# Mask operations pinned in program order, half of the early masks moved beside h, and separate buffers for u

**Chip, cores, metric.** One core of one Trainium2 chip. The metric is the device time in microseconds (us) of that core. The kernel before takes 2171.65 us, the median of its four runs beside the changed kernel (2167.68 to 2175.49). Every run that this document compares is of the fast state, except one single look whose state is unknown, which is marked. A ratio is the mean time of one kernel's fast runs over the mean time of the other's fast runs of the same rounds, so it is not quite the ratio of the medians that are quoted.

## The reference

Two layers of a graph network on 4096 nodes with 512 features, adjacency `adj` 4096 x 4096 in float32:

```python
xw  = max(sign(x), 0) @ sign(W0).T                 # binary weights
x   = layernorm(x + relu(adj @ xw))                # "aggregation"
node_att = softmax(x @ node_w, axis=0)
h   = x @ edge_w                                   # "h"
e   = where(adj > 0, h @ h.T, -9e15)               # "scores e"
att = node_att * softmax(e, axis=1)
x   = layernorm(x + adj * att @ (x @ weight) + bias)   # "final product"
```

The places where `adj` is not positive have to be known when the scores are made. Part of these masks is made early: a piece of `adj` (128 rows x 1024 columns, 512 KB) is loaded, turned into bf16 zeros and large negative numbers (256 KB), and stored in a DRAM tensor `mask_d`, from which the stage of e reads it later. There are 80 such early pieces. The rest of `adj` is loaded and masked during e.

## The kernel before

A compiler with a scheduler orders the instructions of each engine. It may move an operation ahead of others that stand before it in the program, unless that operation is pinned with `keep_in_program_order`. Names: PE is TensorE, DVE is VectorE, ACT is ScalarE, POOL is GpSimd, SP is SyncE. "The wire" is what the DMA engines can carry together; the DMA share is the mean share of time in which they were busy, and the clock is the granted clock of PE as a share of full speed.

The aggregation takes blocks of 128 rows of `adj_t`. Each block has two halves of two quarters. ACT makes a high part `hi` of a quarter, DVE the remainder `lo`, and PE multiplies both:

```python
pieces = deque((r, j, c) for r in range(NG) for j in range(BG) for c in range(0, r + 1, 2))   # 80
bufs = deque([pair[:, 0, :], pair[:, 1, :], single])       # three buffers of 512 KB
def premask():
    if loaded and (len(loaded) == 2 or not pieces):
        (r, j, c), a = loaded.popleft()
        m = a.bitcast(BF16)...[:, :, :W]                   # the mask lies in the piece's own buffer
        nc.vector.tensor_scalar(m, a..., 0.0, NEG_BIG, ALU.is_le, ALU.mult)
        nc.gpsimd.dma_start(mask_d[r][:, c : c + 2, j, :], m)
        bufs.append(a)
    if pieces:
        r, j, c = pieces.popleft()
        a = bufs.popleft()
        nc.gpsimd.dma_start(a, adj[ts(r * BG + j, P), c * W : (c + 2) * W])
        loaded.append(((r, j, c), a))

def aggregate(b):
    ...
    for half in range(2):
        nc.sync.dma_start(at, adj_t[b, :, ts(half, HB), :])       # 1 MB
        for q in range(2):
            nc.scalar.copy(hi, aq)
            nc.vector.tensor_sub(lo, aq, hi.bitcast(F32))
            if (half, q) != (0, 0):
                premask()
            ... 16 matmuls of hi and lo against xw, into acc
    nc.vector.scalar_tensor_tensor(xb, acc, 0.0, xb, ALU.max, ALU.add)
    layernorm([xb]); ... sums and stores on GpSimd ...
```

Before it stands the head: the product `xw`, with the first two blocks beside it, whose loads `a` shared four buffers (`rows`) with `u`, an intermediate result of the binary product. After it stands h, a dense run of 56 groups of matmuls in which the DMA engines had next to nothing to do (11 GB/s at a share of 0.03).

Of the kernel before, what the change touches and what calls it, by code (L numbers as in the profile page):

```python
# [11 lines left out]
F32 = mybir.dt.float32  # L12
# [3 lines left out]
ALU = mybir.AluOpType  # L16
AX = mybir.AxisListType

P = 128
EPS = 1e-5  # L20
NEG_BIG = -(2.0**53)
# [7 lines left out]
def kernel(  # L29
# [13 lines left out]
    nc = tc.nc  # L43
    N, D = x.shape
    NB = N // P
    KD = D // P
    W = 512
    NG = N // W
    BG = W // P
# [7 lines left out]
    rows = ctx.enter_context(tc.tile_pool(name="rows", bufs=4))  # L57
# [98 lines left out]
    with (  # L156
# [15 lines left out]
        def whole(g):  # L172

            xt = stream.tile([P, KD, W], F32, name="xt", tag="stream")
            ba = wp.tile([P, KD, W // 2], F32R, name="ba", tag="quarter", bufs=2)
            pws = [ps_mm.tile([P, D], F32, name="pw", tag="mm") for j in range(BG // 2)]
            order = [(k, j) for j in range(BG // 2) for k in range(KD)]

            def signs(k, over):
                a, b = xt[:, k, : W // 2], xt[:, k, W // 2 :]  # L180
                nc.vector.tensor_scalar(over, b, 0.0, TWO, ALU.is_gt, ALU.mult)
                nc.vector.scalar_tensor_tensor(ba[:, k, :], a, 0.0, over, ALU.is_gt, ALU.add)

            if g == 0:

                pos = sp.tile([P, KD, D], BF16, name="pos", tag="lo")
                over = sp.tile([P, KD, W // 2], F32, name="over0", tag="hi")
                for k in range(KD):
                    nc.sync.dma_start(w0[:, k, :], w0_t[ts(k, P), :])
                    nc.scalar.dma_start(xt[:, k, :], x_t[ts(k, P), ts(g, W)])  # L190
                for _ in range(WARM):
                    nc.tensor.matmul(pws[0], warm[:, :P], warm, start=True, stop=True)
                for k in range(KD):
                    nc.vector.tensor_scalar(pos[:, k, :], w0[:, k, :], 0.0, None, ALU.is_gt)
                    signs(k, over[:, k, :])
                    nc.vector.scalar_tensor_tensor(bw[:, k, :], w0[:, k, :], 0.0, pos[:, k, :], ALU.is_lt, ALU.subtract)
                order = [(k, j) for k in range(KD) for j in range(BG // 2)]
            else:
                nc.sync.dma_start(xt, x_t[:, ts(g, W)].rearrange("(k p) n -> p k n", p=P))
                over = sp.tile([P, KD, W // 2], F32, name="over0", tag="hi")  # L200
                nc.vector.tensor_scalar(over, xt[:, :, W // 2 :], 0.0, TWO, ALU.is_gt, ALU.mult)
                nc.vector.scalar_tensor_tensor(ba, xt[:, :, : W // 2], 0.0, over, ALU.is_gt, ALU.add)
            for k, j in order:
                nc.tensor.matmul(pws[j], ba[:, k, ts(j, P)], bw[:, k, :], start=(k == 0), stop=(k == KD - 1))
                if k == KD - 1:

                    u = rows.tile([P, D], F32, name="u", tag="rows")
                    nc.scalar.activation(u, pws[j], AF.Identity, bias=shift[:, 0:1])
                    b = g * BG + j
                    nc.vector.scalar_tensor_tensor(xw[:, b, :], u, SHIFT, pws[j], ALU.subtract, ALU.subtract)  # L210
                    nc.scalar.activation(xw[:, b + BG // 2, :], u, AF.Identity, bias=shift[:, 1:2], scale=-1.0 / TWO)
# [38 lines left out]



        pieces = deque((r, j, c) for r in range(NG) for j in range(BG) for c in range(0, r + 1, 2))
        pair = wp.tile([P, 2, 2 * W], F32, name="pair", tag="we_s")
        single = wp.tile([P, 2 * W], F32, name="single", tag="quarter", bufs=2)
        sums_l = wp.tile([P, 4, HD], F32, name="sums_l", tag="quarter", bufs=2)
        bufs = deque([pair[:, 0, :], pair[:, 1, :], single])
        loaded = deque()

        def premask():  # L260

            if loaded and (len(loaded) == 2 or not pieces):
                (r, j, c), a = loaded.popleft()

                m = a.bitcast(BF16).rearrange("p (c w) -> p c w", c=2)[:, :, :W]
                nc.vector.tensor_scalar(m, a.rearrange("p (c w) -> p c w", c=2), 0.0, NEG_BIG, ALU.is_le, ALU.mult)  # L266
                nc.gpsimd.dma_start(mask_d[r][:, c : c + 2, j, :], m)
                bufs.append(a)
            if pieces:
                r, j, c = pieces.popleft()  # L270
                a = bufs.popleft()
                nc.gpsimd.dma_start(a, adj[ts(r * BG + j, P), c * W : (c + 2) * W])
                loaded.append(((r, j, c), a))


        def aggregate(b):
            xb = rows.tile([P, D], F32, name="xb", tag="rows")
            nc.sync.dma_start(xb, x[ts(b, P), :])
            acc = accs[early.index(b)] if b in early else ps_mm.tile([P, D], F32, name="acc", tag="mm")
            for half in range(0 if b in early else 2):  # L280
                at = stream.tile([P, HB, P], F32, name="at", tag="stream")
                nc.sync.dma_start(at, adj_t[b, :, ts(half, HB), :])

                for q in range(2):
                    aq = at[:, ts(q, QC), :]
                    hi = sp.tile([P, QC, P], F32R, name="hi", tag="hi")
                    nc.scalar.copy(hi, aq)  # L287
                    lo = sp.tile([P, QC, P], F32R, name="lo", tag="lo")
                    nc.vector.tensor_sub(lo, aq, hi.bitcast(F32))  # L289
                    if (half, q) != (0, 0):  # L290
                        premask()
                    for c in range(QC):
                        kb = half * HB + q * QC + c
                        nc.tensor.matmul(acc, hi[:, c, :], xw[:, kb, :], start=(kb == 0), stop=False)  # L294
                        nc.tensor.matmul(acc, lo[:, c, :], xw[:, kb, :], start=False, stop=(kb == NB - 1))  # L295
            nc.vector.scalar_tensor_tensor(xb, acc, 0.0, xb, ALU.max, ALU.add)
            layernorm([xb])
            scr = wp.tile([P, D], F32, name="scr")
            nc.vector.tensor_tensor_reduce(
                scr, xb, nw_b, 1.0, 0.0, ALU.mult, ALU.add, accum_out=node_s[:, b : b + 1]  # L300
            )
            nc.gpsimd.tensor_add(scr, xb, bias_b)
            nc.gpsimd.dma_start(x1_d[ts(b, P), :], scr)
            return xb
# [22 lines left out]
        for n in range(NB):  # L327
            b = n // 2 + n % 2 * HB
            xb = aggregate(b)
            if n == NB - 3:  # L330
                assert not loaded
                we_s = wp.tile([P, KD, D], F32, name="we_s")
                nc.sync.dma_start(we_s, edge_w.rearrange("(k p) o -> p k o", p=P))
            if n % 2:
                left(n // 2, before[1], xb)
            if before is not None:
                transpose_rows(*before)
            before = (b, xb)
# [12 lines left out]
        nc.gpsimd.tensor_sub(s3, l11, l21)  # L351
        nc.gpsimd.tensor_sub(s4, l12, s2)
        left_h = l11, l12, s4, l22, s1, s2, s3
        for g in range(HG):
            r11, r12 = (x1T[:, :HK, ts(c, W)] for c in (g, g + HG))
            r21, r22 = (x1T[:, HK:, ts(c, W)] for c in (g, g + HG))
            t1, t2 = (sp.tile([P, HK, W], F32, name="t12", tag="hi") for _ in range(2))
            t3, t4 = (sp.tile([P, HK, W], F32, name="t34", tag="lo") for _ in range(2))
            nc.vector.tensor_sub(t1, r12, r11)
            nc.gpsimd.tensor_sub(t3, r22, r12)  # L360
            nc.vector.tensor_sub(t2, r22, t1)
            nc.vector.tensor_sub(t4, r21, t2)
            right_h = r11, r21, r22, t4, t1, t2, t3
            seven(
                lambda m, q: [left_h[m][:, k, ts(q, P)] for k in range(HK)],
                lambda m: [right_h[m][:, k, :] for k in range(HK)],
                [[hT[:, q + f, ts(c, W)] for f in (0, HK) for c in (g, g + HG)] for q in range(2)],
                lambda *_: None,
            )


    nmax = const.tile([P, 1], F32, name="nmax")
# [98 lines left out]
    class Rows:  # L471
# [24 lines left out]
        def row(self, i, s, src):  # L496
            b, c = self.r * BG + i, self.c
            if self.i is None:
                e = Uses(1, free_e)
                line, mask = e.buf, self.mask[:, i, :]  # L500
            else:
                e = self.a
                line = mask = e.buf.rearrange("p c w -> p (c w)")
                nc.vector.tensor_scalar(mask, mask, 0.0, NEG_BIG, ALU.is_le, ALU.mult)  # L504
            nc.vector.tensor_tensor_reduce(  # L505
                line, mask, src, -1.0, HUGE, ALU.add, ALU.min, accum_out=nmax_c[:, b, c : c + 1]
            )
# [534 lines left out]
```

## Time and profile before

The stages are cut at the first or last matmul of each; the head ends where DVE takes over the first accumulator after the two early blocks.

| stage | us | what limits it |
|---|---|---|
| head | 103.2 | PE 77 us busy, waits for `hi` |
| aggregation | 583.2 | 16 blocks of 24.1 us with four or five masks each (72 in all), then 15.0 us per block |
| h | 96.4 | PE |
| e | 495.6 | PE, idle 20 us |
| final product | 894.6 | PE |
| span of the profiled execution | 2173.0 | |

The prediction below shows the windows, the waits of PE and DVE in the aggregation, and one stall. Three more answers matter. The last two I used in the prediction; the first I had not weighed. It is what GpSimd waited for between 103.2 and 489.5 us (total us, times, longest):

```profile
POOL pair L272 <- DMA mask_d<-pair: 80.1, 24, 8.9
POOL single L272 <- DMA mask_d<-single: 36.1, 8, 7.7
```

Both lines say that GpSimd, about to issue the load of a piece, stood until the store of the mask out of the same buffer had landed: 116 us of 386. In the longest of these waits, the 8.87 us before 114.56 us, the trace shows no instruction of GpSimd start: what stands behind such a load waits too. Then the head (PE, 0 to 103 us) and the stage of e (DVE, 783 to 1278 us):

```profile
PE acc L234 <- ACT hi L224: 17.0, 8, 7.5
```
```profile
DVE lent L504 <- DMA lent<-in_adj_dram: 91.6, 36, 5.8
```

### The profile page before, as it was taken

What the parts mean: (1) busy time and instruction counts of PE and PEld (TensorE: products, weight loads), DVE (VectorE), ACT (ScalarE), POOL (GpSimd) and SP (SyncE); (2) the same over time, 40 slices, a digit from 0 to 9 for tenths busy, and PEclk for the clock granted to TensorE, in tenths of its full rate; (3) what the DMA queues carried; (4) which work ended last, traced back from release to release, by engine and by line L of the source; (5) the groups of instructions that cost most, each with busy time, mean ns of one, the idle gap of its engine ahead of it and who ended that gap; (6) DMA issues with size and microseconds to landing.
All of it is one profiled execution on the core that took longest, in us unless ns stands there. A gap on an engine that the chain in (4) does not pass through costs nothing.

```text
span 2173.0 us, 18035 instructions
## 1 busy us (share of the span) xinstructions
PE 2015.5 (93%) x6108; PEld 1119.2 (52%) x6108; DVE 1340.4 (62%) x1896; ACT 672.3 (31%) x1107; POOL 555.7 (26%) x683
## 2 busy tenths in 40 slices
PE   6867767779999999989999989999999999999997
PEld 4646656657886444544454544444444444444443
DVE  5544444535556545746674668778777867686734
ACT  3411212222332035756665752112111211121100
POOL 0345444543334100111111221124022411241101
PEclk8988988889999999999999999999999999999999
DMA  6778888787662045856784987776667665766531
GB/s 232 252 273 283 282 276 289 272 277 249 205 210 84 0 160 189 287 207 240 267 296 159 363 313 283 247 259 227 238 208 278 229 230 208 274 245 232 174 106 58
DMA packets 133644, 497.70 MB, mean 229 GB/s; under 512 B 14000, under 2 KB 14000, under 8 KB 125872
## 3 DMA queue, kind: packets, MB, share of 16 engines
q0 software_dynamic: 83008, 304.12, 38.9%
q1 hardware_dynamic: 49968, 191.39, 26.7%
q8 instruction: 48, 0.79, 0.1%
q10 hardware_dynamic: 576, 1.05, 0.1%
q14 instruction: 44, 0.36, 0.0%
HBM read 376.96 MB, written 119.54 MB: 228 GB/s over the span
## 4 chain that ended last, share of the span: by engine, by line
PE 46%; DMA 4%; issue 3%; DVE 2%; POOL 0%; ACT 0%; POOLq 0%; DVEq 0%
PE ps L828 35%; PE seven L642 5%; PE po L881 4%; DMA s_d<-slot 1%; DMA lent<-in_adj_dram 1%; DVE line L505 1%; DMA s_d<-lent 1%; PE pt L543 1%; DMA lent<-in_adj_t_dram 0%; DMA slot<-in_adj_t_dram 0%; DVE lent L505 0%; DMA xb<-x_d 0%; ACT line L514 0%; DVE lent L504 0%; POOL s_d L659 0%
## 5 line engine op out<-in xcount | busy, mean ns | idle before, releaser
L295 PE MATMUL acc<-xw,lo 128*128 128x512 f32 x960 | 402.3, 419 | 101.2 <-DVE lo L289 101.1
L828 PE MATMUL ps<-lent,lop 128*128 128x512 f32 x992 | 432.6, 592 | 0.0
L294 PE MATMUL acc<-xw,hi 128*128 128x512 f32 x960 | 397.4, 414 | 0.0
L828 PE MATMUL ps<-slot,lop 128*128 128x512 f32 x800 | 351.9, 594 | 0.0
L828 PEld LDWEIGHTS ps<-lent,lop 128*128 128x128 f32 x992 | 188.3, 190 | 236.3 <-issue 231.3
L295 PEld LDWEIGHTS acc<-xw,lo 128*128 128x128 f32 x960 | 194.1, 202 | 158.1 <-DVE lo L289 116.4
L828 PEld LDWEIGHTS ps<-slot,lop 128*128 128x128 f32 x800 | 152.2, 191 | 190.1 <-issue 185.4
L287 ACT CAST hi<-at 128x1024 fp32r<-128x1024 f32 x120 | 125.8, 1048 | 304.0 <-PE acc L294 296.3
L294 PEld LDWEIGHTS acc<-xw,hi 128*128 128x128 f32 x960 | 194.1, 202 | 40.7
L289 DVE TENSOR_TENSOR lo<-at,hi 128x1024 fp32r<-128x1024 f32 x120 | 153.8, 1284 | 57.4 <-ACT hi L287 57.3
L832 DVE TENSOR_TENSOR over<-over,ps 128x512 f32<-128x512 f32 x168 | 113.3, 680 | 92.4 <-PE ps L828 92.4
L266 DVE TENSOR_SCALAR pair<-pair 128x1024 bf16<-128x1024 f32 x54 | 43.3, 802 | 154.1 <-DMA pair<-in_adj_dram 138.9
L573 PE MATMUL pe<-hT 128*128 128x512 f32 (+3 forms) x384 | 134.7, 493 | 0.0
L514 ACT ACTIVATE line<-line,nmax_c 128x512 f32<-128x512 f32 x160 | 114.9, 724 | 58.8 <-DVE nmax_c L505 58.6
L745 ACT ACTIVATE slot<-slot 128x2048 f32<-128x2048 f32 x31 | 59.3, 1912 | 205.5 <-DVE slot L742 205.5
L745 ACT ACTIVATE lent<-lent 128x2048 f32<-128x2048 f32 x33 | 62.9, 1910 | 188.2 <-DVE lent L742 184.1
L881 PE MATMUL po<-over 128*128 128x512 f32 x256 | 114.2, 592 | 3.2 <-DVE xb L890 3.2
L151 ACT ACTIVATE rstd<-mv,eps 128x1 f32<-128x1 f32 (+1 forms) x43 | 12.6, 295 | 315.3 <-DVE mv L149 315.3
L742 DVE CUSTOM_DVE_ANT_1 slot<-slot,line 128x2048 f32<-128x2048 f32 x31 | 73.0, 2356 | 49.1 <-DMA slot<-s_d 49.1
L505 DVE CUSTOM_DVE_ANT_0 line<-lent,slot 128x512 f32<-128x512 bf16 x144 | 92.0, 686 | 15.2 <-ACT slot L544 9.5
L742 DVE CUSTOM_DVE_ANT_1 lent<-lent,line 128x2048 f32<-128x2048 f32 x33 | 83.0, 2519 | 25.9 <-DMA lent<-s_d 24.7
L642 PE MATMUL seven<-hT 128*128 128x512 f32 x192 | 89.7, 594 | 0.0
(193 smaller groups left out, 2695.8 us busy)
## 6 DMA issues: line engine op xcount, KB each, us to landing
at<-in_adj_t_dram SPq DMA_DIRECT2D x60, 1024.0 KB, 6.6
lop<-lop_d SPq DMA_DIRECT2D x112, 512.0 KB, 3.8
lent<-in_adj_t_dram POOLq DMA_DIRECT2D x35, 1024.0 KB, 7.1
s_d<-slot POOLq DMA_DIRECT2D x34, 1024.0 KB, 5.5
lent<-s_d POOLq DMA_DIRECT2D x33, 1024.0 KB, 7.6
slot<-s_d POOLq DMA_DIRECT2D x31, 1024.0 KB, 7.8
slot<-in_adj_t_dram POOLq DMA_DIRECT2D x29, 1024.0 KB, 7.3
pair<-in_adj_dram POOLq DMA_DIRECT2D x54, 512.0 KB, 6.7
```

What stands on the lines that cost most here:

```text
L287: nc.scalar.copy(hi, aq)
L289: nc.vector.tensor_sub(lo, aq, hi.bitcast(F32))
L294: nc.tensor.matmul(acc, hi[:, c, :], xw[:, kb, :], start=(kb == 0), stop=False)
L295: nc.tensor.matmul(acc, lo[:, c, :], xw[:, kb, :], start=False, stop=(kb == NB - 1))
L505: nc.vector.tensor_tensor_reduce(line, mask, src, -1.0, HUGE, ALU.add, ALU.min, accum_out=nmax_c[:, b, c : c + 1])
L514: nc.scalar.activation(line, line, AF.Exp, bias=nmax_c[:, b, c : c + 1], scale=-1.0, accum_out=sum_c[:, b, c : c + 1])
L573: nc.tensor.matmul(pe[:, lo * P :], hT[:, k, ts(A * BG + i, P)], hT[:, k, (B * BG + lo) * P : (B + 1) * W], start=(k == 0), stop=(k == KD ...
L642: nc.tensor.matmul(ps, left[m][:, k, q, :], right[m][:, k, :], start=(first and k == 0), stop=(k == KD // 2 - 1), skip_group_check=not first,)
L742: nc.vector._custom_dve(TENSOR_ADD_SAT, out=q, in0=q, in1=mrow.unsqueeze(1).to_broadcast([P, BG, W]), s0=0.0, s1=-HUGE)
L745: nc.scalar.activation(q, q, AF.Exp)
L828: nc.tensor.matmul(ps, lop[:, c, ts(h, P)], rop[:, c, :], start=(c == 0), stop=(c == BG - 1))
L881: nc.tensor.matmul(po, (lower if k // 2 else upper)[:, k % 2, ts(i, P)], w1_s[:, k, :], start=(k == 0), stop=(k == KD - 1),)
```

## The change

Its intent: keep DVE from standing at masks whose pieces have not landed, by pinning them late enough in the order; move half of the 80 pieces into h, where the wire is empty (11 GB/s); and give `u` buffers of its own. Cut to its core:

```diff
-   u = rows.tile([P, D], F32, name="u", tag="rows")
+   u = wp.tile([P, D], F32, name="u", bufs=2)
...
-   pieces = deque((r, j, c) for r in range(NG) for j in range(BG) for c in range(0, r + 1, 2))
+   pieces = deque((r, j, c) for r in (0, 1, 4, 5, 6, 7, 2, 3) for j in range(BG) for c in range(0, r + 1, 2))
...
-   def premask():
-       if loaded and (len(loaded) == 2 or not pieces):
+   def premask(queue, left):
+       if loaded and (len(bufs) == 1 or len(pieces) == left):
...
-           nc.vector.tensor_scalar(m, a..., 0.0, NEG_BIG, ALU.is_le, ALU.mult)
+           tc.keep_in_program_order(nc.vector.tensor_scalar(m, a_, 0.0, NEG_BIG, ALU.is_le, ALU.mult))
...
-       if pieces:
+       if len(pieces) > left:
...
-           nc.gpsimd.dma_start(a, adj[...])
+           queue.dma_start(a, adj[...])
...   # in the aggregation
-           if (half, q) != (0, 0):
-               premask()
+           if q == 0:
+               premask(nc.gpsimd, 40)
...   # in h: two 1 MB stream buffers as four, and single, make five
+   more = [stream.tile([P, 2, 2 * W], F32, name="more", tag="stream") for _ in range(2)]
+   bufs.extend(m[:, n, :] for m in more for n in range(2))
+   for _ in range(4):
+       premask(nc.sync, 0)
+   def between_h(q, n):                       # between the groups of matmuls of h
+       count[0] += q is None
+       if q is None and count[0] > 6:
+           premask(nc.sync, 0)
...   # the remaining masks of e
-   nc.vector.tensor_scalar(mask, mask, 0.0, NEG_BIG, ALU.is_le, ALU.mult)
+   tc.keep_in_program_order(nc.vector.tensor_scalar(mask, mask, 0.0, NEG_BIG, ALU.is_le, ALU.mult))
```

More of the change, by code (lines that the diff above doesn't have):

```diff
@@ L258 @@
         loaded = deque()
-        def premask():
-            if loaded and (len(loaded) == 2 or not pieces):
+        def premask(queue, left):
+            if loaded and (len(bufs) == 1 or len(pieces) == left):
                 (r, j, c), a = loaded.popleft()
                 m = a.bitcast(BF16).rearrange("p (c w) -> p c w", c=2)[:, :, :W]
-                nc.vector.tensor_scalar(m, a.rearrange("p (c w) -> p c w", c=2), 0.0, NEG_BIG, ALU.is_le, ALU.mult)
+                a_ = a.rearrange("p (c w) -> p c w", c=2)
+                tc.keep_in_program_order(nc.vector.tensor_scalar(m, a_, 0.0, NEG_BIG, ALU.is_le, ALU.mult))
                 nc.gpsimd.dma_start(mask_d[r][:, c : c + 2, j, :], m)
                 bufs.append(a)
-            if pieces:
+            if len(pieces) > left:
                 r, j, c = pieces.popleft()
                 a = bufs.popleft()
-                nc.gpsimd.dma_start(a, adj[ts(r * BG + j, P), c * W : (c + 2) * W])
+                queue.dma_start(a, adj[ts(r * BG + j, P), c * W : (c + 2) * W])
                 loaded.append(((r, j, c), a))
@@ L331 @@
                 assert not loaded
+                bufs.clear()
+                bufs.append(single)
                 we_s = wp.tile([P, KD, D], F32, name="we_s")
@@ L353 @@
         left_h = l11, l12, s4, l22, s1, s2, s3
+        more = [stream.tile([P, 2, 2 * W], F32, name="more", tag="stream") for _ in range(2)]
+        bufs.extend(m[:, n, :] for m in more for n in range(2))
+        for _ in range(4):
+            premask(nc.sync, 0)
+        count = [0]
+        def between_h(q, n):
+            count[0] += q is None
+            if q is None and count[0] > 6:
+                premask(nc.sync, 0)
         for g in range(HG):
@@ L367 @@
                 [[hT[:, q + f, ts(c, W)] for f in (0, HK) for c in (g, g + HG)] for q in range(2)],
-                lambda *_: None,
+                between_h,
             )
+        assert not loaded and not pieces
     nmax = const.tile([P, 1], F32, name="nmax")
```

## The prediction

> **What bounds the kernel now.** I read the page's busy shares first, then a table of windows cut at the stage boundaries (taken from the first and last matmul of each source line), then who waited for whom inside the slow stage, then the timeline of one stall.
>
> ```profile
> 0.00:103.20 103.20, 76.74 (x275) 54.39 (x276) 56.98 (x91) 40.05 (x59) 17.33 (x26) 0.88 0.70 237
> 103.20:489.50 386.30, 288.59 (x1109) 224.39 (x1107) 179.92 (x249) 79.23 (x98) 182.14 (x243) 0.87 0.82 279
> 489.50:686.30 196.80, 194.22 (x867) 159.94 (x868) 113.17 (x148) 62.14 (x75) 81.35 (x87) 0.98 0.60 200
> 686.30:783.30 97.00, 96.89 (x232) 43.00 (x231) 49.38 (x67) 12.42 (x22) 14.36 (x15) 1.00 0.03 11
> 783.30:1278.40 495.10, 475.36 (x1562) 245.75 (x1561) 304.11 (x641) 311.07 (x693) 70.13 (x112) 0.99 0.71 253
> 1278.40:2173.00 894.60, 883.68 (x2073) 391.75 (x2072) 636.85 (x706) 167.35 (x162) 190.41 (x201) 1.00 0.64 223
> ```
> Columns: stretch, length, busy time of PE, PE loads, DVE, ACT, POOL, then the granted PE clock, DMA share, GB/s. The rows are: first product and two early blocks; aggregation with masks being made; aggregation after the last mask; h; the scores e; the final product. Only the second row is far from PE-bound: PE idle 98 us, clock 0.87. In h the DMA carries 11 GB/s: an empty wire.
>
> The times at which DVE takes over an accumulator give the period of a block of 128 rows. From 103.2 to 489.5 us there are 16 periods: 24.1 us each. From 489.5 to 686.3 they come 15.0 us apart (506.0, 521.0, 536.0 ...) with the same 64 matmuls: that is PE's own pace, and this half of the stage shows it reached. So the masks cost up to 16 x 9.1 = 147 us. Why:
>
> ```profile
> PE acc L295 <- DVE lo L289: 94.3, 29, 7.7
> ```
> ```profile
> DVE pair L266 <- DMA pair<-in_adj_dram: 129.2, 43, 8.5
> DVE single L266 <- DMA single<-in_adj_dram: 53.6, 23, 7.3
> DVE pair L266 <- DMA single<-in_adj_dram: 8.1, 1, 8.1
> DVE pair L266 <- DMA mask_d<-pair: 7.1, 1, 7.1
> DVE lo L289 <- ACT hi L287: 5.9, 5, 2.8
> ```
> These are the waits of PE and of DVE in 103 to 490 us (total, times, longest). PE waits for `lo`, which DVE makes; DVE waits almost only for mask pieces to land, 198 us in all. One such stall:
>
> ```profile
> 289.06 1.23 DVE L289 TENSOR_TENSOR lo<-at,hi 128x1024 fp32r<-128x1024 f32 x1 [0.25 <-ACT hi L287]
> 297.85 0.69 DVE L266 TENSOR_SCALAR pair<-pair 128x1024 bf16<-128x1024 f32 x1 [7.56 <-DMA pair<-in_adj_dram]
> 298.46 0.68 DVE L296 SCALAR_TENSOR_TENSOR xb<-acc,xb 128x512 f32<-128x512 f32 x1
> 301.05 0.69 DVE L266 TENSOR_SCALAR single<-single 128x1024 bf16<-128x1024 f32 x1 [1.90 <-DMA single<-in_adj_dram]
> 301.66 0.69 DVE L148 BATCH_NORM_STATS2 stats<-xb 128x6 f32<-128x512 f32 x1
> 302.26 1.21 DVE L289 TENSOR_TENSOR lo<-at,hi 128x1024 fp32r<-128x1024 f32 x1
> ```
> ```profile
> 303.52 0.80 PE L295 MATMUL acc<-xw,lo 128*128 128x512 f32 x1 [6.60 <-DVE lo L289]
> 304.12 0.63 PE L294 MATMUL acc<-xw,hi 128*128 128x512 f32 x1
> 304.54 0.63 PE L295 MATMUL acc<-xw,lo 128*128 128x512 f32 x1
> ```
> DVE stands at a mask operation whose 512 KB have not landed, `lo` stands behind it, PE starves 6.6 us, and then its matmuls start 0.43 us apart instead of 0.23 for 3 us. The program asked for three mask operations per block at most; the compiled order of before has five in most blocks (80 pieces are used up after 16 of 30 blocks), since the scheduler floats them ahead.
>
> [...] `lo` at 302.26 started behind a mask operation although its own inputs were ready. [...] 0.43 against 0.23 us for seven matmuls. So a stall costs more than its length: 94 us of waits made 147 us of periods. [...] 279 GB/s at share 0.82, so a full wire is estimated at 279/0.82 = 340. [...]
>
> **The change part by part.** I compared the compiled orders of both kernels.
>
> 1. *Masks during the aggregation.* Now 40 pieces instead of 80, two per block at quarter 0 of each half, pinned in written order. A load now has two calls, each half a block (7.5 us), so 15 us, to land, against the median 6.7 us of `pair` loads. The DVE waits on masks should fall from 198 us to near 0. Bytes per block: 2 MiB of adj_t (2.10 MB), x 0.26, x1 0.26, left operands 0.46, two pieces at 0.52 + 0.26 = 1.57: 4.65 MB. At PE's pace of 15.0 us this is 310 GB/s, 91% of my 340. So the wire is close to binding, and I choose 15.4 us for the 20 blocks with masks, 15.0 for the 9 without: 20 x 15.4 + 9 x 15.0 = 443 us for what took 686.3 - 103.2 = 583.1. **-140 us.** The buffers of the row loads and of adj_t do not change here.
>
> 2. *Own buffers for u.* In the first 103 us PE waits 17.0 us (8 times) for `hi`, i.e. for the loads of `a`, whose four buffers were shared with `u`. The new order on SP's queue puts these loads one group earlier. No mask piece disturbs this stretch any more either. But the share of DMA is already 0.70 there. I take a third of the 17.0: **-5 us.**
>
> 3. *40 pieces during h.* h is 97 us of dense PE work, 56 calls 1.7 us apart. Pinned DVE work added: 40 x 0.69 = 28 us onto 49 us busy: fits in 97. The wire: 40 x 0.79 MB = 31.5 MB; at 340 GB/s 93 us. The five buffers: load about 5 us to land, mask 0.7, store issued on POOL and landed about 5 us, issue gaps 1 to 2: an estimated 12 to 13 us per five pieces, with the first stores held by POOL's subtraction `t`, which itself waits for PE about 23 us into h (it ran at 709.5 before). So the last of seven further rounds is masked about 23 + 7 x 12.5 = 110 us after h starts. In the compiled order of DVE the last mask stands just ahead of the additions of m4 in the fourth group; those of the groups before ran at 706.2, 730.2 and 754.3 us, so the fourth's at about 778.3, 92 us after h starts. [...] the additions behind late masks slip[...]. 110 - 92 - 5 = 13 us, and a PE stall here may add slow matmuls[...]. I choose **+14 us**.
>
> 4. *Mask operations of e in written order.* DVE waits 91.6 us (36 times) there for `lent`, pieces of adj, and PE loses 495.1 - 475.4 = 19.7 us in the whole stage. A wait moved to a later position is shorter, but it does not always hold PE up. I take a quarter: **-5 us**.
>
> 5. *Final product.* 1278 to 2173 us is PE-bound at clock 1.00 and untouched: 0.
>
> Sum: -140 - 5 + 14 - 5 = -136; 2171.5 - 136 = **2035 us** (0.937).
>
> **The rivals.** (a) *The wire is the bound.* If the mixed traffic does not exceed the 280 GB/s it has now, a block with masks takes 4.65/0.279 = 16.7 us, 26 us more than I chose over 20 blocks, and h needs 31.5/0.279 = 113 us for its masks plus some 10 of start, 12 more than I chose: 2073. For: share 0.82, mean slices hardly above 300. Against: single slices of before reach 356 GB/s; and DVE's waits also limited what was asked. (b) *h takes back what the aggregation gives:* a piece late in a pinned place holds the additions, PE stalls[...]. At three stalls per group of 3 us each with the slow matmuls after them h grows by 40 to 50 us: 2065. For: five buffers are barely enough by my count. (c) *Nothing waits in either:* 15.0 us per block, h at 97, the head gains 10 and e 10: 2171 - 148 - 20 = 2003. (d) *The masks were hidden anyway,* and PE would then wait for adj_t instead: no gain, 2170. Against: the 200 us of aggregation after the last mask run at 15.0 us with no wait of PE; the three 1 MB buffers suffice there at 200 GB/s.
>
> **Range and chances.** Aggregation -148 to -115, h 0 to +45, head 0 to -10, e -12 to +8. They are mostly independent, so I take 2005 to 2075. Even all bad ends together (2171 - 115 + 45 + 8 = 2109) are under 2128, the 2% line. Faster 0.97, same 0.02, slower 0.01.
>
> **What would show each step right or wrong.** Step 1: block periods of 15.0 to 15.8 us, DVE's waits for `pair` and `single` under 20 us, clock near 1.00, DMA share about 0.9. Periods of 16.5 or more with waits of `hi` for adj_t would mean rival (a). Step 2: waits of PE for `hi` in the head about 10 us. Step 3: DVE waits for `more` of some tens of us, h 105 to 125 us; 97 means I oversized it, 140 rival (b). Step 4: DVE waits for `lent` in e below 60 us, PE idle about 15. The final product should stay within 3 us of 895. The prediction is wrong as a whole if a new wait appears at the start of e, for instance because `lent` buffers come free later after the masks of h.

## The result and the profile after

The changed kernel takes 2093.59 us, the median of four runs (2085.59 to 2096.94), ratio 0.9635 with a 95% interval of 0.9601 to 0.9669. It is faster by 78 us. The prediction was 2035 us, within 2005 to 2075: right in direction and wrong in size.

The windows of the changed kernel, with the same columns as in the prediction (length, busy time of PE, PE loads, DVE, ACT, POOL; then clock, DMA share, GB/s): head, aggregation with masks, aggregation after them, h, e, final product.

```profile
0.00:80.10 80.10, 71.46 (x274) 51.53 (x275) 54.66 (x86) 39.49 (x59) 13.67 (x22) 0.94 0.86 297
80.10:458.10 378.00, 324.74 (x1362) 260.97 (x1361) 220.24 (x260) 98.11 (x121) 149.68 (x196) 0.93 0.70 242
458.10:593.30 135.20, 135.20 (x615) 111.77 (x614) 78.15 (x100) 43.60 (x53) 56.40 (x57) 1.00 0.60 204
593.30:720.50 127.20, 104.79 (x231) 44.35 (x230) 76.62 (x106) 12.52 (x22) 45.43 (x55) 0.93 0.68 235
720.50:1200.10 479.60, 470.69 (x1561) 244.40 (x1560) 307.17 (x643) 311.60 (x693) 69.43 (x112) 1.00 0.73 261
1200.10:2094.00 893.90, 883.77 (x2073) 391.89 (x2073) 640.22 (x706) 167.70 (x162) 191.80 (x201) 1.00 0.63 223
```

| stage | before | after | measured difference | predicted |
|---|---|---|---|---|
| head | 103.2 | 80.1 | -23.1 | -5 |
| aggregation | 583.2 | 513.3 | -69.9 | -140 |
| h | 96.4 | 126.8 | +30.4 | +14 |
| e | 495.6 | 480.0 | -15.6 | -5 |
| final product | 894.6 | 893.8 | -0.8 | 0 |
| span | 2173.0 | 2094.0 | -79.0 | -136 |

The second window answers for the largest miss. Twenty blocks carry masks and take 378.0 us, so 18.9 us each, where I had chosen 15.4; the DMA share is 0.70, lower than before, which speaks against the wire as the reason (the kernel with masks out of place, below, settles it). The first four of these blocks last 15.0 to 16.3 us, the others 16.9 to 23.5. What each engine waited for in those other sixteen (143 to 458 us):

```profile
POOL pair L274 <- DMA mask_d<-pair: 119.9, 20, 10.4
POOL single L274 <- DMA mask_d<-single: 63.4, 10, 10.0
PE acc L297 <- DVE lo L291: 52.2, 15, 5.9
DVE pair L268 <- DMA pair<-in_adj_dram: 26.5, 6, 6.1
DVE single L268 <- DMA single<-in_adj_dram: 19.0, 4, 6.7
DVE scr L301 <- DMA x_d<-scr: 17.0, 16, 2.5
```

GpSimd stands 183 of 315 us at loads of pieces whose buffer's store has not landed; DVE still waits 45 us for pieces and 17 us for the store of `scr`; PE loses 52 us to `lo`. One turn of the buffer `single`, first DVE's two operations on it, then GpSimd between them:

```profile
288.28 0.68 DVE L268 TENSOR_SCALAR single<-single 128x1024 bf16<-128x1024 f32 x1
...
319.44 0.69 DVE L268 TENSOR_SCALAR single<-single 128x1024 bf16<-128x1024 f32 x1 [6.68 <-DMA single<-in_adj_dram]
```
```profile
290.86 0.56 POOL L274 DMA_DIRECT2D pair<-in_adj_dram  x1 [5.67 <-DMA mask_d<-pair]
291.41 0.74 POOL L269 DMA_DIRECT2D mask_d<-pair  x1
296.37 0.56 POOL L274 DMA_DIRECT2D pair<-in_adj_dram  x1 [4.22 <-DMA mask_d<-pair]
...
303.39 0.71 POOL L269 DMA_DIRECT2D mask_d<-single  x1
314.14 0.56 POOL L274 DMA_DIRECT2D single<-in_adj_dram  x1 [10.04 <-DMA mask_d<-single]
```

The mask is made at 288.28. Its store is issued only at 303.39, 15.1 us later, because GpSimd stood in between for the two stores of `pair` and then worked off the sums of a block. The store lands 10.8 us later, and only then the next load into this buffer is issued, which DVE can use at 319.44. A turn of 31 us. Two pieces per block of 15.0 us out of three buffers allow 1.5 blocks, 22.5 us. This buffer is late by 9 us, and DVE pays 6.7 of them at a pinned operation with the next `lo` behind it.

The kernel before had shown such an order on DVE: `lo` at 302.26 started behind a mask operation that had waited 1.90 us for its piece. I used this for DVE and did not look for it on GpSimd. The trace shows it there too: nothing of GpSimd started in the 10.04 us before 314.14.

In h (593 to 721 us) the answering waits are

```profile
DVE more L268 <- DMA more<-in_adj_dram: 38.6, 17, 7.1
PE seven L98 <- DVE hT L113: 14.1, 3, 6.7
```

DVE stands 39 us at pieces that have not landed, the additions `hT` behind them are late, and the PE clock falls to 0.93. The last mask was made at 717.6, 124 us after the start of h; I had reckoned with 110.

In the head, PE's wait for `hi` is gone from the list of waits, and the DMA engines move 297 GB/s there instead of 237. In e the waits of DVE for `lent` pieces (91.6 us) no longer appear in the list, and PE is idle 8.9 us instead of 19.7.

### The profile page after: what moved, and what is told of

Same layout as the page of the kernel before. It is cut to its first block, busy times and chain, and to the rows that moved or that the text cites. A ratio compares the mean times of both kernels' runs of the same rounds, so it can differ in the third digit from the quotient of the medians.

```text
span 2094.0 us, 18051 instructions
## 1 busy us (share of the span) xinstructions
PE 1990.7 (95%) x6108; PEld 1104.9 (53%) x6108; DVE 1377.1 (66%) x1896; ACT 673.0 (32%) x1107; POOL 526.4 (25%) x643
## 4 chain that ended last, share of the span: by engine, by line
PE 70%; DMA 14%; issue 6%; POOL 5%; DVE 4%; ACT 1%; POOLq 0%; DVEq 0%; SPq 0%; ACTq 0%
PE ps L846 37%; PE seven L660 11%; PE acc L297 5%; PE acc L296 5%; PE po L899 5%; DMA mask_d<-pair 4%; DMA more<-in_adj_dram 2%; PE pe L591 2%; DMA mask_d<-single 2%; PE pt L561 2%; PE seven L98 1%; DMA s_d<-slot 1%; POOL scr L304 1%; DVE lo L291 1%; DMA mask_d<-more 1%
## 5 line engine op out<-in xcount | busy, mean ns | idle before, releaser
L297 PE MATMUL acc<-xw,lo 128*128 128x512 f32 x960 | 389.6, 406 | 55.6 <-DVE lo L291 55.6
L296 PE MATMUL acc<-xw,hi 128*128 128x512 f32 x960 | 388.9, 405 | 0.0
L291 DVE TENSOR_TENSOR lo<-at,hi 128x1024 fp32r<-128x1024 f32 x120 | 183.3, 1528 | 116.5 <-ACT hi L289 116.5
L297 PEld LDWEIGHTS acc<-xw,lo 128*128 128x128 f32 x960 | 188.2, 196 | 103.2 <-DVE lo L291 63.7
L296 PEld LDWEIGHTS acc<-xw,hi 128*128 128x128 f32 x960 | 188.0, 196 | 39.1
L760 DVE CUSTOM_DVE_ANT_1 lent<-lent,line 128x2048 f32<-128x2048 f32 x33 | 82.9, 2518 | 24.8 <-DMA lent<-s_d 23.5
L561 PEld LDWEIGHTS pt<-ident,lent 128*128 128x128 f32 x422 | 52.5, 142 | 62.2 <-issue 40.1
```

The source lines that it names most:

```text
L296: nc.tensor.matmul(acc, hi[:, c, :], xw[:, kb, :], start=(kb == 0), stop=False)
L297: nc.tensor.matmul(acc, lo[:, c, :], xw[:, kb, :], start=False, stop=(kb == NB - 1))
L760: nc.vector._custom_dve(TENSOR_ADD_SAT, out=q, in0=q, in1=mrow.unsqueeze(1).to_broadcast([P, BG, W]), s0=0.0, s1=-HUGE)
```

## The experiments

Twelve kernels ran, in three groups, each on a chip of its own and with its own runs of the kernel before (medians 2175.99, 2173.43 and 2172.22 us). The record marks all results as correct, also that of the one kernel that was meant to be wrong on purpose; why the check let it pass is not known. Each figure of a stage is read from the trace as in the table above.

### Parts alone

**Only the buffers of u**, on the kernel before:

```diff
-   u = rows.tile([P, D], F32, name="u", tag="rows")
+   u = wp.tile([P, D], F32, name="u", bufs=2)
```

> The kernel before with only the buffers of u taken apart. In the changed kernel the head (up to the first block taken over after the two early ones) ended at 80.1 us instead of 103.2. Theory: u's own buffers let the rows of adj_t be loaded a group earlier, so the head ends near 83 us and the kernel gains 15 to 23 us (ratio 0.990 to 0.993). Rival: the head gained because no mask operation and no mask transfer lies in it any more; then this kernel gains under 6 us.

2146.95 us, ratio 0.9873 (0.9849 to 0.9897). The head falls to 82.2 us and PE's waits for `hi` vanish from it; the aggregation takes 577.5, all else is as before. So the head's gain belongs to this one line, and it is more than the 17.0 us that PE had waited: PE's busy time in the head also falls, from 76.7 to 71.2 us for the same matmuls, while the granted clock of that window rises from 0.88 to 0.94.

**Only the pin of the early masks**, on the kernel before (80 pieces, three calls per block):

```diff
-   nc.vector.tensor_scalar(m, a..., 0.0, NEG_BIG, ALU.is_le, ALU.mult)
+   tc.keep_in_program_order(nc.vector.tensor_scalar(m, a..., 0.0, NEG_BIG, ALU.is_le, ALU.mult))
```

> The kernel before with only its early mask operations kept in written order (all 80 pieces stay in the aggregation, three per block, u and the rest as before). Theory S: the changed kernel's blocks take 18.9 us because GpSimd's in-order queue stands at each load of a piece until the store out of the same buffer has landed (183 of 315 us). With three pieces per block that is three landings of about 6 us plus 4 us of own work, so about 22 us per block over 27 blocks: 590 us or more, no gain, total 2160 to 2210. Rival P: it is the pin that gains, since DVE no longer stands at pieces that have not landed; then the wire sets the pace, 5.4 MB at 340 GB/s = 16 us per block, 430 us for 27 blocks, total 2030 to 2060.

2146.9 us, ratio 0.9872 (0.9836 to 0.9907): between the two theories. The aggregation takes 562.8 us, 20 less than before, now with masks in nearly all blocks, whose periods alternate between 15.0 and up to 28 us. The pin is worth something, but far from what I had put on it.

**Only the pin of the masks of e**, on the kernel before:

```diff
-   nc.vector.tensor_scalar(mask, mask, 0.0, NEG_BIG, ALU.is_le, ALU.mult)
+   tc.keep_in_program_order(nc.vector.tensor_scalar(mask, mask, 0.0, NEG_BIG, ALU.is_le, ALU.mult))
```

> The kernel before with only the mask operations of the couples (stage e) kept in written order. In the changed kernel e took 479.6 us instead of 495.1. Theory: that is this pin, so e takes about 480 us, DVE's waits for pieces of adj there fall from 92 us to under 50, and the kernel gains 10 to 16 us (ratio 0.993 to 0.995). Rival: e gained by what came before it (masks of rows 2 and 3 made later, other order), then this kernel is within 4 us of before.

2157.26 us, ratio 0.9927 (0.99 to 0.9953). e takes 479.3 us, which is the whole gain of that stage in the changed kernel.

### What holds up the aggregation

**The masks out of place.** The changed kernel, but in the aggregation a mask is written into another buffer, so that a piece's buffer is free as soon as DVE has read it. Two buffers take loads; the third, cut in two, and a new one of 256 KB take masks:

```diff
+   third = wp.tile([P, 2 * W], BF16, name="third")
+   outs = deque([single.bitcast(BF16)[:, : 2 * W], single.bitcast(BF16)[:, 2 * W :], third])
-   bufs = deque([pair[:, 0, :], pair[:, 1, :], single])
+   bufs = deque([pair[:, 0, :], pair[:, 1, :]])
...
-       if loaded and (len(bufs) == 1 or len(pieces) == left):
+       if loaded and (len(bufs) == (queue is nc.sync) or len(pieces) == left):
+           if queue is nc.gpsimd:
+               m = outs[0]...; outs.rotate(-1)
```

> The changed kernel, but the 40 masks of the aggregation are written to three small buffers of their own (two in the third load buffer's place), so the two load buffers are free as soon as DVE has read them, and no load waits for a store to land. Bytes, queues and number of pieces are unchanged. Theory S (the queue standing at the store's landing): GpSimd's waits for mask stores fall from 183 us to under 30, the blocks with masks take 15.0 to 16.2 us instead of 18.9, the stage gains 50 to 75 us, total 2020 to 2045. Rival W (the wire, share 0.70 in bursts, or adj_t arriving late): blocks stay at 18 to 19 us, total 2085 to 2095.

2015.32 us, ratio 0.9269 (0.9243 to 0.9295). All 27 full blocks last 15.0 us; the aggregation takes 435.1 us. Theory S held, and the gain lies just beyond the range that I gave for it. Its windows, with masks and after them:

```profile
75.80:376.40 300.60, 300.60 (x1368) 248.85 (x1366) 209.29 (x261) 100.66 (x122) 166.12 (x198) 1.00 0.88 308
376.40:510.90 134.50, 134.50 (x611) 111.05 (x610) 77.59 (x99) 42.80 (x52) 55.95 (x57) 1.00 0.61 208
```

PE is busy for all of it. The wire carries 308 GB/s at a share of 0.88, with the same bytes from the same queues; I had worked out 310 GB/s at 91%. So rival W, and the prediction's rival that the wire limits the mixed traffic to 280 GB/s, are refuted. The loads of `pair` land more slowly now (median 8.5 us against 4.5), but they are issued early: DVE waits only 1.4 us for them in 143 to 458 us. In 143 to 458 us the waits of GpSimd for a store before a load, 183 us in the changed kernel, are gone from the list.

**The order of the queue alone.** The changed kernel, masks in place, with the stores and loads of pieces pinned in written order, so that a load comes one call after the store of its buffer and not right behind it:

```diff
-   nc.gpsimd.dma_start(mask_d[r][:, c : c + 2, j, :], m)
+   put = nc.gpsimd.dma_start(mask_d[r][:, c : c + 2, j, :], m)
+   if queue is nc.gpsimd: tc.keep_in_program_order(put)
...   # the load likewise
```

> The changed kernel (masks in place) with the loads and stores of the aggregation's pieces kept in written order on GpSimd's queue too. There each store is followed by the load into the buffer whose store went out one call (7.5 us) earlier, not by the load into its own. Theory S1 (it was the scheduler's order, load straight behind the store of the same buffer, that made the queue stand): GpSimd's waits for mask stores fall from 183 us to under 60, blocks at 15 to 16.5 us, total 2020 to 2050. Rival S2 (it is writing in place as such: both calls of a block lie next to each other on the queue, so a landing is still waited for once per block): waits of 60 to 120 us, blocks at 16.5 to 18 us, total 2050 to 2085.

2088.61 us, ratio 0.9603 (0.958 to 0.9625): slightly above the upper end. GpSimd's waits for stores in 145 to 458 us shrink to a third (the last two lines):

```profile
POOL sums_l L318 <- DVE xb L154: 57.8, 8, 8.2
POOL pair L276 <- DMA mask_d<-pair: 40.7, 11, 6.9
POOL single L276 <- DMA mask_d<-single: 18.0, 5, 5.3
```

but the aggregation takes 504.3 us, only 9 less. GpSimd still waits for a store 16 times in 16 blocks, as rival S2 had it. And now it stands 108 us in 17 places at its sums until DVE has made `xb` (the first line and a like one of 49.9 us), where the changed kernel shows 0.3 us of this; pieces stand behind that. DVE waits 68 us for pieces or stores at its masks. So this run does not show how much a better order alone would bring. My reading, argued and not shown, is that a buffer that is written in place needs its load, its mask operation and its store to land before the next load, and that three such buffers are too few at this pace. Masks out of place take away both, the waits for stores and the long turn. That kernel also has more pieces of memory (two for loads and three for masks); how much comes from their number alone was not separated, because no run gives the aggregation more or larger buffers with its masks in place.

**The pin taken away, in place and out of place.** In both, only the masks of the aggregation lose the pin:

```diff
-   tc.keep_in_program_order(nc.vector.tensor_scalar(m, a_, 0.0, NEG_BIG, ALU.is_le, ALU.mult))
+   mk = nc.vector.tensor_scalar(m, a_, 0.0, NEG_BIG, ALU.is_le, ALU.mult)
+   if queue is nc.sync: tc.keep_in_program_order(mk)
```

> The changed kernel with the pin of the mask operations of the aggregation taken away (those of h and e stay pinned). If the pin is what took DVE's waits for pieces from 198 us to some 55: they come back, blocks with masks last 20 to 23 us, total 2105 to 2135. Rival (the landing of stores on GpSimd's queue sets the pace with or without the pin): DVE's waits differ, but the total stays within 8 us of the changed kernel's 2094.

> The version with masks out of place, with the pin of the mask operations of the aggregation taken away. If the pin still matters once no load waits for a store: DVE stands at pieces, blocks longer than 15.5 us, total 2030 to 2070. Rival (the pin does nothing once the in-place wait is gone): blocks at 15.0 us, total within 5 us of 2015.

Without the pin: 2088.49 us in place (ratio 0.9616, 0.9598 to 0.9635) and 2080.77 us out of place (0.9583, 0.9561 to 0.9604). With the two kernels before them this makes a table of four:

| masks of the aggregation | floating | pinned |
|---|---|---|
| in place | 504.0 us (run: 2088.5) | 513.3 us (run: 2093.6) |
| out of place | 492.5 us (run: 2080.8) | 435.1 us (run: 2015.3) |

(The aggregation, and the median of the runs.) In place, the pin is worth nothing: the rival held. Out of place it is worth 57 us of the stage. Of the two expectations for the second kernel, that of a pin that still matters held, at 2081 beyond the range that I gave. Neither half of the remedy does much alone. The windows of the blocks with masks, floating in place and floating out of place:

```profile
80.30:269.00 188.70, 144.28 (x565) 112.99 (x563) 90.52 (x125) 40.55 (x50) 92.41 (x124) 0.88 0.84 290
```
```profile
83.30:261.50 178.20, 137.47 (x543) 106.55 (x544) 91.36 (x126) 39.03 (x48) 88.03 (x120) 0.92 0.87 296
```

There the scheduler packs 36 of the 40 masks into eight blocks, five and four in turn, which then last 23.6 and 22.3 us on average; the blocks after them last 15.0. By these lines 6.8 and 6.6 MB were moved per block; in 15.0 us this would be some 440 to 455 GB/s, and the busiest 20 us that I found in the traces of this case carried 410 (the kernel before had 407 from 1205 to 1225 us). So blocks packed in this way would have needed more than any stretch here shows. What set their actual length is open: the DMA share is 0.84 and 0.87, high but no higher than the 0.88 of the kernel in which nothing waits, and DVE stands 73 and 83 us there at pieces that have not landed. A busy wire and the small number of load buffers could both make them late. The pin spreads the same bytes over twenty blocks, two masks in each. The kernel before, with four or five pieces per block and 279 GB/s, may have had the same limit; no run shows it.

### What holds up h

**Stores alone.** The changed kernel, in h neither loads nor masks, only 40 stores of zeros; its result is wrong on purpose:

```diff
+   if queue is nc.sync:
+       if len(pieces) > left:
+           r, j, c = pieces.popleft()
+           nc.gpsimd.dma_start(mask_d[r][:, c : c + 2, j, :], zero...)
+       return
```

> Wrong result on purpose: in h only the stores of the masks remain (zeros from one buffer), no loads and no mask operations of DVE; the aggregation is that of the changed kernel. Theory: the 30 us that h grew by come from DVE standing at pieces that have not landed, so h is back at 97 us and the total near 2064. Rival: the memory traffic of the stores, or GpSimd, slows h by itself; then h stays over 105 us.

One look, its state unknown: 2085.8 us. h takes 96.5 us, as before. But the run does not test what it was built for. The stores of zeros wait for no load and no mask, and they are not pinned, so the scheduler moved all 40 of them to the start of the kernel (first and last start, in us):

```profile
L267 POOL DMA_DIRECT2D mask_d<-zero x40: 725/725/1070, 2.1 to 42.0; - x40
```

None is left in h, which moves 11 GB/s as in the kernel before. So this run shows nothing about stores in h; whether they or GpSimd's work on them slow h by themselves stays untested. It also fits this kernel's long head of 99.6 us: the wire carried 405 GB/s from 8 to 58 us, and DVE waited 15.6 us in the head for loads of `x_t`.

**The masks of h out of place**, into three buffers of 256 KB, with five loads ahead of h:

```diff
+   outs = deque([wp.tile([P, W], F32, name="third"), *(wp.tile([P, W], F32, name="u", bufs=2) for _ in range(2))])
...   # in h
+   m = outs[0]...; outs.rotate(-1)
```

> The changed kernel, the aggregation untouched, but the 40 masks of h are written to three buffers of their own (those of u and one more), so that the five load buffers are free when DVE has read them. Theory T (turnaround: load, mask, store, landing, then the next load, about 14 us per round of five buffers): h falls from 127 to 100 to 112 us. Rival V (the wire: share 0.87 to 0.89 in the second half of h): h stays at 118 to 127 us.

2093.41 us, ratio 0.9631 (0.9611 to 0.965): no gain. h takes 124.4 us instead of 126.8. DVE no longer waits for pieces but for the stores out of the three output buffers:

```profile
DVE u L272 <- DMA mask_d<-u: 15.5, 11, 4.4
DVE third L272 <- DMA mask_d<-third: 11.2, 8, 4.5
```

So the turn of a buffer in place is not shown to be what limits h. My theory fell here (rival V's range held), or at least these three buffers are the next limit at nearly the same place.

**The all-reduces later.** In the changed kernel GpSimd starts nothing for 7.5, 10.3 and 10.3 us at three places in h, each just ahead of an all-reduce over the partitions (for the node attention, which nobody needs yet) or of the next plain subtraction after one, and stores of masks stand behind that. Here they are pinned behind the masks of h:

```diff
-   nc.vector.tensor_reduce(nmax, node_s, AX.X, ALU.max)
+   tc.keep_in_program_order(nc.vector.tensor_reduce(nmax, node_s, AX.X, ALU.max))
```

> The changed kernel with the maximum and the sum over all partitions [...] kept behind h, where they are written, instead of in its first 40 us. In the changed kernel GpSimd stood 7.5 and 10.3 us around them with mask stores queued behind. Theory: stores go out earlier in the first two rounds, h falls by 8 to 20 us. Rival: the second half of h, at 300 GB/s, sets the pace; then under 5 us.

2086.63 us, ratio 0.9598 (0.9582 to 0.9614); h takes 120.5 us, 6 less, between the theory and its rival. A part of the cause, not the main one.

**Fewer pieces in h.** Out of place, and 52 pieces in the aggregation, whose last blocks have room, with 28 in h; then the same with the all-reduces later:

```diff
-   premask(nc.gpsimd, 40)
+   premask(nc.gpsimd, 28)
```

> The version with masks out of place during the aggregation, with 52 pieces there and 28 in h (40 and 40 before). Theory (h grows with the pieces that are left for it, because DVE stands at pieces that have not landed, while the aggregation at 15.0 us per block has room for pieces in its remaining blocks): blocks stay at 15.0 to 15.3 us, h falls from 128 to 105 to 115 us, total 1995 to 2006 us. Rival (the growth of h is a start-up cost of its loads, not the count): h stays above 120 us, total 2010 to 2016. Second rival (the wire is full in blocks with masks, at 0.88): the six further blocks with masks get slower than 15.5 us and the total does not fall.

> As the balanced version, with the two all-reduces on GpSimd pinned behind the mask operations of h. Theory (the all-reduces hold back the stores of masks in h for 10 us each, so loads come late): a further 2 to 6 us less in h. Rival (with 28 pieces there is slack enough): within 2 us of the balanced version. It can also lose, if something in e needs the all-reduces early.

2003.08 us (ratio 0.9221, 0.9203 to 0.9239) and 1999.78 us (0.9207, 0.9189 to 0.9225). The aggregation stays at 15.0 us per block (435.3 and 435.1 us) and h takes 114.4 and 110.7 us: both theories held. The windows of the second kernel, blocks with masks and h:

```profile
76.70:466.00 389.30, 389.30 (x1768) 322.22 (x1767) 271.34 (x337) 129.56 (x156) 214.07 (x258) 1.00 0.88 308
511.80:622.50 110.70, 99.72 (x230) 42.37 (x229) 65.68 (x91) 10.84 (x19) 34.53 (x41) 0.98 0.53 185
```

With 0, 28 and 40 pieces (the first figure is of the run with nothing in h) it takes 96.5, 114.4 and 128.5 us: the last 12 pieces cost 14.1 us, 1.2 us each, where the aggregation takes them for nothing. The second kernel, at 1999.78 us, is the fastest of all, 94 us under the changed kernel by the medians.

## Why the prediction was wrong

**Step 1, the masks during the aggregation, -140 predicted, -69.9 measured.** This is the step that failed, and the sentence in it is "A load now has two calls, each half a block (7.5 us), so 15 us, to land". It counts from the place in the program. The load is not issued there: it stands on GpSimd until the store of its own buffer has landed (183 of 315 us in such waits), and that store stands behind other such loads. So the term "15.4 us for the 20 blocks" measured 18.9, 70 us too little in the sum. What stands in its place, by the four kernels of the table, is that with 40 pieces the pin pays only when a load needn't wait for a store. (With 80 pieces, in place, the pin alone shortened the stage by 20 us.) With the waits for stores gone the same step, bytes and all, gives what I predicted for it and more: 435 us against my 443.

What the stage did gain came from fewer pieces, not from the pin: the buffers of `u` alone give -5.7 us (583.2 to 577.5), with 40 pieces fewer and floating masks it takes 504.0, and the pin adds 9.3. My sign for step 1 (DVE's waits for pieces under 20 us, DMA share 0.9) failed with 45 us in sixteen blocks and 0.70, and holds in the kernel out of place. Sorting the waits of the kernel before by GpSimd would have shown 116 us of this wait; I asked only PE and DVE, because GpSimd was busy half of the time and seemed far from the bound. Two readings beside it were off as well: the masks in 16 blocks were 72, four and five in turn and not five in most, and 340 GB/s is not a full wire for every kind of traffic (in its e the changed kernel carried 383 GB/s from 1115 to 1165 us, at share 1.00). Neither made the miss.

**Step 2, u, -5 predicted, -23.1 measured.** Right in mechanism and too small. I held the head back by its DMA share of 0.70 and took a third of the wait. The share rose to 0.86, and u alone brought 21.0 us of it: 15.5 us of PE's idle time (the 17.0 us of waits for `hi` are gone, some others grew) and 5.5 us of its busy time.

**Step 3, h, +14 predicted, +30.4 measured.** The mechanism is right: landings that DVE waits for at pinned places, additions behind them, PE late. The term was mis-sized: the last mask came 124 us after the start, not 110. The landings of about 5 us in it were near the medians of the kernel before (6.7 and 5.0 us for loads of `pair` and `single`, 4.9 and 5.3 us for the stores of their masks). Nor is the last mask alone what counts, as my sum "110 - 92 - 5" had it, in which the 5 us, a slack of PE, was my estimate and was not shown: with the all-reduces later it comes 109 us after the start, just as I predicted, and h still grows by 24 us, for PE has been held by `hT` several times before (3.0 us at 46, 5.6 us at 70, 4.0 us at 105 us after the start). Two causes are shown in part: the all-reduces on GpSimd (6 us), and the number of pieces (the last 12 cost 14 us). That the turn of the buffers in place is the cause was my reading, and the run with other output buffers did not confirm it. What would bound 40 pieces in h if not the buffers was only argued: 40 x 0.79 MB at the 300 to 308 GB/s of busy stretches are 102 to 105 us, where I had taken 93 at 340. The changed kernel carries 303 to 305 GB/s from 60 to 120 us after the start of h, but only 66, 211 and 209 in the three stretches of 20 us before, so the wire is at most the limit of the second half.

**Step 4, e, -5 predicted, -15.6 measured.** Right in kind: the pin alone gives it (16.3 us). I took a quarter of PE's idle time of 19.7 us; 10.8 us of it went, and 4.7 us of PE's busy time too (475.4 to 470.7 for the same matmuls).

**Step 5, the final product,** was right: -0.8 us.

**The rivals.** (a) the wire at 280 GB/s came nearest to the result with 2073 us, for a wrong reason: 308 GB/s were carried once nothing stood. (b) h taking back 40 to 50 us is half true, with 30. (c) 2003 us, with nothing waiting anywhere, is what the rebalanced kernel reached, by luck: its h takes 114.4 us and not 97, and its head and e gain more than 10 each. (d) is refuted. The errors of head and e, 29 us in my favour together, hid part of the 70 us of step 1. My range assumed that aggregation could lose no more than 33 us against its best; it lost 78.

## What to carry to other kernels

When a buffer is loaded, worked on in place and stored from again, count the whole turn, and count it from when the queue's engine can issue, not from the written line; here a load that waited for a store held what stood behind it on GpSimd, up to 10.4 us at a time and 183 of 315 us in all. Pinning a consumer and freeing its producer belong together: here the pin alone gave nothing (5 us more, within the noise of the two ratios), the free buffer alone gave 8, and both together gave 73 (medians, against neither). A pin may also help by spreading transfers evenly (out of place, twenty blocks of 15.0 us with it, and without it eight of 22.3 us on average), so look how many a scheduler has packed into one block before blaming either the wire or the wait. And look in the trace of a test kernel whether the scheduler left the operations where the test needs them.

## What the traces show of landings, GpSimd and the wire

- A store of 256 KB took 4.7 to 6.2 us from issue to landing (medians by buffer, in the kernel before, the changed kernel and the one with masks out of place), and single loads behind one stood 10.4 us.
- A load behind a store of its own buffer held up other stores and arithmetic on GpSimd: 183 of 315 us in the changed kernel.
- In the kernel before GpSimd starts nothing for 6.7 us ahead of the subtraction after the first all-reduce and for 5.9 us ahead of the second all-reduce, and the trace shows nothing that it waited for. So such gaps stand both where GpSimd goes from an all-reduce to a plain operation and where it goes back; what fills them is not shown. In the changed kernel, with the wire busy, the gaps at these places are 7.5 to 10.3 us; the profile puts two of them down to a load, so their cause is not settled.
- The changed kernel carried 383 GB/s from 1115 to 1165 us, and the kernel with the zeros 405 GB/s from 8 to 58 us. The mixed traffic of the aggregation stayed below that: 308 GB/s over 389 us in which PE never starved.
